# A graph attention kernel on one core: the last stage cut into 25 units, most of them run between the last steps of the edge loop

## The chip, the core and the metric

The kernel runs on one core of a Trainium2 chip. Its engines are TensorE (PE in the profile, its weight loads PEld), VectorE (DVE), ScalarE (ACT), GpSimd (POOL) and SyncE (SP), each with its own instruction stream, worked off in order. SyncE, ScalarE and GpSimd also issue DMA transfers, which 16 DMA engines carry out. The metric is the device time of one execution, in microseconds, as a median of several.

## The reference

There are 12,500 nodes with 128 features and 400,000 edges, sorted by their target node. Node rows are normalized, cut at zero, and multiplied by two weight matrices. Each edge adds the rows of its source and target, multiplies them by a small network's output on its 32 edge features and by its weight, and gives eight attention scores and eight value vectors. A softmax over all edges of a target weighs the values, which are summed per target, projected, and added to x:

```
h = maximum(layernorm(x), 0)
message = (h @ w_src + b_src)[src] + (h @ w_dst)[dst]
message = (message * edge_weight * mlp(edge_attr)) @ w_sep + b_sep
score = einsum(smooth_leaky_relu(message[:, :, :16]), alpha_dot)
att = exp(score - max[dst]) / (sum of exp over the target's edges + 1e-16)
out = segment_sum(message[:, :, 16:] * att, dst)
return x + out @ w_proj + b_proj
```

## The kernel before

**Node stage.** The rows of x are normalized and multiplied, and the tables t_src and t_dst are written to memory. The function fits checks that the targets are sorted and that no section of 512 edges spans more than 63 targets; its result, bad, chooses between the fast path (windows) and a slow one that never runs on these inputs.

**Edge loop.** In windows a step k handles two sections of 512 edges; there are NP = 391 steps. GpSimd gathers source rows two steps ahead. Transposes, the network, the message and the scores follow. The softmax needs maxima over eight steps, so the values are made LAG = 13 steps later: for c = k - 13, values multiplies and weighs, one_hot builds a selection matrix, and sums adds each section's edges into its window of 64 targets (tile ob, three buffers). store_win writes the whole window of a step to win; store writes 63 rows of each of its two sections to agg, at the row where the section's first target lies. So a step has three such transfers on SyncE's queue. Rows of targets that lie on a section's border come from several sections. They are joined by the block functions: a block takes the 128 border rows of 64 sections out of win (block_rows, tile rr), scales and adds them along the sections (block_maxima to block_totals), and block_out writes the joined rows to obs_d. There are NC = 13 blocks. The first eleven are made within the loop; the last two in the last steps. scatter lets GpSimd write joined rows to agg by an indirect transfer. The order of all this is written out by hand: each engine gets its instructions in the order of the program, and the program only adds the waits.

**The last steps.** Steps 391 to 404 hold what the lag leaves: values, sums and stores of c = 378 to 390, and the last two blocks by the table jobs. Here also the joined rows of the eleven early blocks are loaded from obs_d (tile comb, two buffers), one in each step, and scattered. A store to agg waits for the stores and scatters before it, and a scatter for the stores, since rows may overlap; only stores of the last block's sections (c from 384) are freed from waiting for scatters (declare_no_dep, group "combined"). From step 394 on ScalarE's queue loads x plus bias (xb, made during the loop) into one large tile x_fin, in 7 groups and a rest.

**The final stage.** The function final begins when all is scattered. agg is seen as 97 tiles of 128 nodes and a rest of 84, with node p * 97 + t on partition p. load_g loads agg by twelve tiles (128 partitions of 12 x 136 numbers), quotients divides the sums by the eight totals, turn transposes four tiles and copies them, finish multiplies them by w_proj, adds x_fin and writes the output.

Of the kernel before, what the change touches and what calls it, by code (L numbers as in the profile page):

```python
# [30 lines left out]
P = 128  # L31
C = 128
# [24 lines left out]
def gnn_kernel(ctx: ExitStack, tc: tile.TileContext, a: dict, out: bass.AP):  # L57
# [9 lines left out]
    NX = -(-NP // MP) * MP * PR  # L67
    assert NT * P == E and RC * RP == E and NT % TPI == 0 and NT % SORT_T == 0
# [88 lines left out]
    with tc.tile_pool(name="node", bufs=2) as np_, tc.tile_pool(name="node1", bufs=1) as n1, \  # L157
# [22 lines left out]
        ends = n1.tile([NH, 17, 2], I32, name="ends")  # L180
        eb = n1.tile([P, NS, 2], I32, name="eb")
# [6 lines left out]
        def load_targets():  # L188

            nc.sync.dma_start(out=cur[:, 1:CC + 1], in_=dst.rearrange("(p c) -> p c", p=P))  # L190
            at = dst[CC - 1:CC]
            with nc.allow_non_contiguous_dma(reason="single targets"):
                nc.sync.dma_start(out=cur[1:P, 0:1], in_=bass.AP(at.tensor, at.offset, [[CC, P - 1], [1, 1]]))
                at = dst[0:1]
# [114 lines left out]
        def fits():  # L309
# [14 lines left out]
            nc.vector.tensor_copy(bad, sum_)  # L324
# [425 lines left out]
    def windows():  # L750
# [7 lines left out]
        with tc.tile_pool(name="ps", bufs=1, space=PSUM) as pp, \  # L758
# [326 lines left out]

            def store(c, f):
                at = nc.sync.value_load(base[0:1, f, c:c + 1])
                st = nc.sync.dma_start(out=agg[ds(at, W - 1), :], in_=accs[c][f * W:(f + 1) * W - 1, :])
                if 2 * c + 1 >= (NC - 1) * (P // 2):
                    tc.declare_no_dep(st.ins, group="combined", reason="its rows follow those of the blocks")  # L1090
# [102 lines left out]
            def scatter(g):  # L1193
                w = width(g)
                st = nc.gpsimd.indirect_dma_start(
                    out=agg[0:N, :], in_=comb[g][:w, :], in_offset=None,
                    out_offset=bass.IndirectOffsetOnAxis(ap=ids[:w, g:g + 1], axis=0),
                    bounds_check=N - 1, oob_is_err=False)
                tc.declare_no_dep(st.ins, group="combined", reason="each node's row is written once")
                tc.add_to_no_dep_group("combined", st.ins)  # L1200

            comb = {}

            def combined(g):
                comb[g] = tail_pool.tile([P, ROW], F32, name="comb", bufs=2)
                return comb[g]
# [12 lines left out]
            def step(k):  # L1219
# [109 lines left out]

            for k in range(-5, NP):  # L1330
                step(k)
            held.close()


            tail_pool = held.enter_context(tc.tile_pool(name="fin1", bufs=1, side="right"))
            x_fin = tail_pool.tile([P, NB, C], F32, name="x_fin")
            x_loads = load_xb(x_fin)
            last = NC - 1

            def out_rows(g):  # L1340
                block_rows_out(g, combined(g))
                scatter(g)

# [9 lines left out]
                10: lambda: out_rows(last - 1),  # L1353
            }
            assert SB * (NC - 1) + LAG + 1 == NP + 7
            for k in range(NP, NP + LAG + 1):
# [4 lines left out]
                if 0 <= j - 2 < NC - 2:  # L1361
                    nc.sync.dma_start(out=combined(j - 2), in_=obs_d[(j - 2) * P:(j - 1) * P, :])
                    scatter(j - 2)
                if j >= 3:
                    next(x_loads, None)
            for _ in x_loads:
                pass
            block_rows(last)
# [4 lines left out]
            with tc.tile_pool(name="fin", bufs=3) as fp:  # L1373
                final(fp, x_fin, lambda i: pp.tile([P, 4, P], F32, name=("pm0", "pm1", "V")[i % 3]),
                      lambda i: pp.tile([P, 4, C], F32, name=("p3", "pa", "m1")[i % 3]))


    XQ = 12
    out_v = out[0:NF * P, :].rearrange("(p t) c -> p t c", t=NF)
    agg_v = agg[0:NF * P, :].rearrange("(p t) c -> p t c", t=NF)  # L1380

    def load_xb(x_fin):

        for t0, t1 in groups:
            nc.scalar.dma_start(out=x_fin[:, t0:t1, :], in_=xb_v[:, t0:t1, :])
            yield
        nc.scalar.dma_start(out=x_fin[:tail, NF, :], in_=xb[NF * P:N, :])
        yield

    def final(fp, x_fin, turned, product):  # L1390
        starts = list(range(0, NB, XQ))
        gs, qs, qTs = {}, {}, {}

        def load_g(i):

            gs[i] = fp.tile([P, XQ, ROW], F32, name="g", bufs=len(starts))
            for n, t0, t1 in blocks(starts[i], min(starts[i] + XQ, NB)):
                o = starts[i]
                nc.sync.dma_start(out=gs[i][:n, t0 - o:t1 - o, :],
                                  in_=agg_v[:, t0:t1, :] if n == P else agg[NF * P:N, :].unsqueeze(1))  # L1400

        def quotients(i):
            r = fp.tile([P, XQ, H], F32, name="r")
            qs[i] = fp.tile([P, XQ, C], F32, name="q")
            g = gs.pop(i)
            for n, t0, t1 in blocks(starts[i], min(starts[i] + XQ, NB)):
                s = slice(t0 - starts[i], t1 - starts[i])
                m = t1 - t0
                nc.vector.tensor_scalar(r[:n, s, :], g[:n, s, C:ROW], 1e-16, None, op0=ALU.add)  # L1409
                nc.vector.reciprocal(r[:n, s, :], r[:n, s, :])  # L1410
                nc.vector.tensor_mul(  # L1411
                    qs[i][:n, s, :].rearrange("p t (h k) -> p (t h) k", h=H),
                    g[:n, s, 0:C].rearrange("p t (h k) -> p t h k", h=H),
                    r[:n, s, :].unsqueeze(3).to_broadcast([n, m, H, C // H]))

        def turn(i):
            t0, t1 = quads[i]
            q, o = qs[t0 // XQ], t0 // XQ * XQ
            pt = turned(i)
            for t in range(t0, t1):  # L1420
                n = rows(t)
                nc.tensor.transpose(pt[:, t - t0, :n], q[:n, t - o, :], ident[:n, :n])  # L1422
            w = (t1 - t0 - 1) * P + rows(t1 - 1)
            qTs[i] = fp.tile([P, 4, P], F32, name="qT")
            nc.scalar.copy(qTs[i].rearrange("p u n -> p (u n)")[:, :w], pt.rearrange("p u n -> p (u n)")[:, :w])

        def finish(i):
            t0, t1 = quads[i]
            qT = qTs.pop(i)
            py = product(i)  # L1430
            for t in range(t0, t1):
                n = rows(t)
                nc.tensor.matmul(py[:n, t - t0, :], qT[:, t - t0, :n], w_proj, start=True, stop=True)  # L1433
            for n, u0, u1 in blocks(t0, t1):
                y = x_fin[:n, u0:u1, :]
                nc.vector.tensor_add(y, py[:n, u0 - t0:u1 - t0, :], y)  # L1436
                nc.sync.dma_start(out=out_v[:, u0:u1, :] if n == P else out[NF * P:N, :].unsqueeze(1), in_=y)

        for i in range(len(starts)):
            load_g(i)  # L1440
        quotients(0)
        turn(0)
        for i in range(Q):
            if i % 3 == 1 and i // 3 + 1 < len(starts):
                quotients(i // 3 + 1)
            if i + 1 < Q:
                turn(i + 1)
            finish(i)

# [4 lines left out]
    with fit.Else():  # L1454
# [23 lines left out]
        with tc.tile_pool(name="fin_b", bufs=3) as fp, tc.tile_pool(name="fin1_b", bufs=1) as f1, \  # L1478
                tc.tile_pool(name="fin_ps", bufs=2, space=PSUM) as fps, tc.manual_schedule():
            x_fin = f1.tile([P, NB, C], F32, name="x_fin")  # L1480
            for _ in load_xb(x_fin):
                pass
            final(fp, x_fin, lambda i: fps.tile([P, 4, P], F32, name="pt"),
                  lambda i: fps.tile([P, 4, C], F32, name="py"))
# [36 lines left out]
```

## Time and profile before

| | us |
|---|---|
| median of 3 runs | 4215.05 (4213.84 to 4223.81) |
| the profiled execution | 4210.53 |
| its span, first to last instruction | 4208.8 |
| busy in it: PE, DVE, ACT, POOL | 3913.5, 3104.8, 1901.2, 3010.2 |

A row of the stretches gives busy time and count of instructions of each engine, then the granted clock of TensorE, the busy share of the 16 DMA engines and what they moved. A row of waits names who waited for whom, the sum in us, how often, and the longest. A row of the timeline gives start, duration, engine and line, operation, out<-in, and in brackets the idle time before it with what ended it; SPq is SyncE's queue, whose rows are DMA issues. Where a row says x2, it spans from the first issue to the end of the second.

### The profile page before, as it was taken

What the parts mean: (1) busy time and instruction counts of PE and PEld (TensorE: products, weight loads), DVE (VectorE), ACT (ScalarE), POOL (GpSimd) and SP (SyncE); (2) the same over time, 40 slices, a digit from 0 to 9 for tenths busy, and PEclk for the clock granted to TensorE, in tenths of its full rate; (3) what the DMA queues carried; (4) which work ended last, traced back from release to release, by engine and by line L of the source; (5) the groups of instructions that cost most, each with busy time, mean ns of one, the idle gap of its engine ahead of it and who ended that gap; (6) DMA issues with size and microseconds to landing.
All of it is one profiled execution on the core that took longest, in us unless ns stands there. A gap on an engine that the chain in (4) does not pass through costs nothing. (4 is left out here: it accounts for less than half of the span.)

```text
span 4208.8 us, 87885 instructions
## 1 busy us (share of the span) xinstructions
PE 3913.5 (93%) x29351; PEld 2388.5 (57%) x29351; DVE 3104.8 (74%) x6187; ACT 1901.2 (45%) x4549; POOL 3010.2 (72%) x3195
## 2 busy tenths in 40 slices
PE   6889999999999999999999999999999999999975
PEld 5345555555555555555555555555555555555554
DVE  5567777777777777777777777777777777777754
ACT  5344444444444444444444444444444444444421
POOL 4777777777777777777777777777777777777710
PEclk8899999999999999999999999999999999999988
DMA  6767776777776776777777776676677776766634
GB/s 238 235 181 183 187 193 178 197 192 180 198 193 178 197 194 185 189 197 190 184 192 192 181 194 185 177 188 183 178 187 187 185 183 181 189 179 182 184 86 161
DMA packets 593333, 783.08 MB, mean 186 GB/s; under 512 B 125553, under 2 KB 392302, under 8 KB 592740
## 3 DMA queue, kind: packets, MB, share of 16 engines
q1 hardware_dynamic: 384786, 514.16, 40.6%
q0 software_dynamic: 100416, 205.44, 23.9%
q10 hardware_dynamic: 107666, 57.76, 4.7%
q8 instruction: 234, 3.83, 0.4%
q14 instruction: 231, 1.89, 0.1%
HBM read 637.83 MB, written 139.30 MB: 185 GB/s over the span
## 5 line engine op out<-in xcount | busy, mean ns | idle before, releaser
L865 POOL DMA_INDIRECT gs<-t_src,idx x3125 | 2972.3, 951 | 969.2 <-issue 807.5
L954 ACT ACTIVATE sl<-pa,c_b_a 128x512 f32<-128x512 f32 x782 | 536.9, 687 | 1018.6 <-PE pa L952 1009.9
L959 DVE SCALAR_TENSOR_TENSOR al<-pa,sl 128x512 f32<-128x512 f32 x782 | 540.5, 691 | 594.3 <-ACT sl L954 582.9
L1063 PEld LDWEIGHTS V<-c_w_v,mT 128*128 128x128 f32 x6048 | 746.8, 194 | 292.3 <-DVE ob L1080 119.1
L1063 PE MATMUL V<-c_w_v,mT 128*128 128x128 f32 x6048 | 879.4, 289 | 0.0
L952 PE MATMUL pa<-mT,c_w_a 128*128 128x512 f32 x1564 | 814.0, 603 | 3.9 <-DVE mT L946 3.6
L1065 DVE TENSOR_TENSOR pvx<-V,Pem 128x512 f32<-128x512 f32 x756 | 519.2, 687 | 243.4 <-PE V L1063 230.3
L932 PEld LDWEIGHTS pm<-ident,gs 128*128 128x128 f32 x3125 | 393.3, 142 | 420.4 <-issue 289.6
L1076 PEld LDWEIGHTS misc<-pvx,oh 128*64 128x64 f32 x6250 | 352.5, 137 | 410.6 <-ACT h L888 394.3
L924 DVE SCALAR_TENSOR_TENSOR rad<-p,c_fc_b,w_b 128x512 f32<-128x512 f32 x782 | 550.3, 745 | 39.4 <-PE p L916 3.7
L1076 PE MATMUL misc<-pvx,oh 128*64 128x136 f32 x6250 | 453.8, 287 | 118.3 <-ACT h L888 108.3
L946 DVE SCALAR_TENSOR_TENSOR mT<-pm,c_b_src,rad 128x512 f32<-128x512 f32 x782 | 550.7, 746 | 4.8 <-PE pm L939 4.8
L902 ACT ACTIVATE h<-p,b 128x512 f32<-128x512 f32 x391 | 287.5, 735 | 419.8 <-PE p L899 369.1
L932 PE MATMUL pm<-ident,gs 128*128 128x128 f32 x3125 | 471.9, 274 | 0.0
L916 PE MATMUL p<-h,w3b 64*128 64x512 f32 x1564 | 405.4, 595 | 11.5 <-ACT h L902 11.5
L939 PE MATMUL pm<-ohT,m 64*128 64x512 bf16 x2346 | 323.3, 382 | 0.0
L985 ACT ACTIVATE Sp<-m,b_s 128x512 f32<-128x512 f32 x192 | 131.9, 687 | 394.2 <-PE m L968 394.2
L884 PE MATMUL m<-eT,w1b 64*128 64x256 f32 x782 | 274.4, 431 | 26.1 <-DVE M L1006 16.7
L884 PE MATMUL misc<-eT,w1b 64*128 64x256 f32 x782 | 274.4, 431 | 0.0
L1049 DVE TENSOR_TENSOR oh<-lane,misc 128x504 f32<-128x504 f32 x391 | 262.3, 671 | 0.0
L899 PE MATMUL p<-h,w2b 64*64 64x256 f32 x3128 | 259.8, 403 | 0.0
L952 PEld LDWEIGHTS pa<-mT,c_w_a 128*128 128x128 f32 x1564 | 241.9, 195 | 21.2 <-DVE mT L946 8.1
(172 smaller groups left out, 3649.1 us busy)
## 6 DMA issues: line engine op xcount, KB each, us to landing
w_b<-in_edge_weight SPq DMA_DIRECT2D x390, 512.0 KB
d_b<-in_dst SPq DMA_DIRECT2D x390, 256.0 KB
gs<-t_src,idx POOLq DMA_INDIRECT x3125
e_t<-in_edge_attr ACTq DMA_DIRECT2D x390, 128.0 KB
sc_d<-Sp SPq DMA_DIRECT2D x192, 256.0 KB
win<-ob SPq DMA_DIRECT2D x391, 68.0 KB
agg<-ob SPq DMA_DIRECT2D x782, 33.5 KB
md<-t_dst SPq DMA_DIRECT2D x782, 32.0 KB
```

The lines of the kernel that those rows point to most:

```text
L865: nc.gpsimd.indirect_dma_start(out=gs[:, t, :], out_offset=None, in_=t_src[:, :], in_offset=bass.IndirectOffsetOnAxis(ap=idx[:, t0 + t:t0 ...
L884: nc.tensor.matmul(p1[q], w1b[s, :], eTs[k][s, :], start=True, stop=True)
L916: nc.tensor.matmul(p3s[k][:, f, 0:SEC], w3b[s, :], h2s[k][s, :], start=True, stop=True)
L924: nc.vector.scalar_tensor_tensor(rad[:, s], p3[:, f, 0:n], b3, w_g[k][:, s], op0=ALU.add, op1=ALU.mult)
L932: nc.tensor.matmul(pms[k, f][:, t * T:(t + 1) * T], gs[:, t, :], ident, start=(t == 0), stop=False, is_transpose=True, skip_group_check=True)
L946: nc.vector.scalar_tensor_tensor(mTs[k][:, s], pms.pop((k, f))[:, 0:n], b_n, rad[:, s], op0=ALU.add, op1=ALU.mult)
L952: nc.tensor.matmul(pa[:, 0:n], w_a, mTs[k][:, f * SEC:f * SEC + n], start=True, stop=True)
L954: nc.scalar.activation(sl[:, 0:n], pa[:, 0:n], AF.Silu, bias=b_a, scale=1.0)
L959: nc.vector.scalar_tensor_tensor(al, pa, 0.25, sl, op0=ALU.mult, op1=ALU.add)
L1063: nc.tensor.matmul(V[:, t, :], mTs[c][:, o:o + T], w_v, start=True, stop=True)
L1065: nc.vector.tensor_mul(pvx[c][:, f, 0:n, 0:C].rearrange("p t (h k) -> p t h k", h=H), V[:, 0:n, :].rearrange("p t (h k) -> p t h k", h=H), ...
L1076: nc.tensor.matmul(acc[f * W:(f + 1) * W, :], ohs[c][:, f * TS + t, :], pvx[c][:, f, t, :], start=(t == 0), stop=(t == n - 1), skip_group_ ...
```

## The change

The final stage becomes 25 units of 500 nodes (class Units). Unit u takes nodes 500 u to 500 u + 499, node 500 u + 4 p + t on partition p, so 125 partitions with four nodes each. For a unit, load_x loads 125 x 512 numbers of x plus bias, load_g 125 x 544 numbers of agg, quotients divides in place, turn transposes and copies, finish multiplies, adds and writes 125 x 512 numbers. x has eight buffers and is loaded three units ahead, g has nine and is loaded up to eight ahead. x and the output go over SyncE's queue, and g over ScalarE's for the first 23 units and SyncE's for the last two.

- 18 of the units run in steps 393 to 404, one and two in turn, behind each step's stores and block work. Two more stand between the last block's parts, three behind its scatter, and two at the very end.
- The joined rows of the eleven early blocks are loaded in steps 385 to 388 (bring), three blocks at a time, into buffers of the edge features that are no longer needed, and all eleven scatters are issued at the end of step 388, behind the last gather.
- order replaces the one group by four. Stores and scatters are sorted by section into three classes (below section 704, below 768, the rest), and one class doesn't wait for another's; units below 20 wait for the first class alone, units 20 to 22 for the first two. Two targets are read from dst in the node stage (lim), and fits sends inputs to the slow path where units 0 to 19 or 0 to 22 could hold nodes of later sections.
- In the last step the last window isn't written to win; two rows of each of its sections' borders go from ob to rr directly (last_rows, last_rows_2).

```diff
+            low = n1.tile([1, 2], F32, name="low")
+            for i, u in enumerate((EARLY_1, EARLY)):
+                nc.vector.tensor_scalar(low[:, i:i + 1], lim[:, i:i + 1], float(u * (N // NU)), None, op0=ALU.is_lt)
+            nc.vector.tensor_add(sum_, low[:, 0:1], sum_)
+            nc.vector.tensor_add(bad, low[:, 1:2], sum_)
...
                 if has(c - 1):
                     sums(c - 1)
                     if k >= NP:
-                        store_win(c - 1)
+                        if k == NP + LAG:
+                            last_rows_2()
+                        else:
+                            store_win(c - 1)
                         store(c - 1, 0)
                         store(c - 1, 1)
...
             for k in range(-5, NP):
                 step(k)
+                if 0 <= k - (NP - 6) < 4:
+                    bring(k - (NP - 6))
+                if k == NP - 3:
+                    for g in range(NC - 2):
+                        scatter(g)
...
+            def last_rows_2():
+                q = width(last) // 2
+                for i in range(2):
+                    nc.sync.dma_start(out=rrs[last][(i + 1) * q - 2:(i + 1) * q, :],
+                                      in_=accs[NP - 1][i * (W - 1):i * (W - 1) + W + 1:W, :])
...
-                if 0 <= j - 2 < NC - 2:
-                    nc.sync.dma_start(out=combined(j - 2), in_=obs_d[(j - 2) * P:(j - 1) * P, :])
-                    scatter(j - 2)
-                if j >= 3:
-                    next(x_loads, None)
...
+                if j == 0:
+                    un.load_x(0, 3)
+                    for u in range(7):
+                        un.load_g(u)
+                if j == 1:
+                    un.quotients(0)
+                    un.quotients(1)
+                    un.turn(0)
+                if j >= 2:
+                    un.run(1 + j % 2, EARLY)
+            un.run(1, EARLY)
             block_columns(last)
+            un.run(1, EARLY)
             block_totals(last)
             out_rows(last)
+            un.run(NU, EARLY)
...
+            un.run(NU, NU)
...
+        def load_x(self, u0, u1):
+            for u in range(u0, min(u1, NU)):
+                self.x[u] = self.pool.tile([UP, UT, C], F32, name="xu", bufs=self.nx)
+                nc.sync.dma_start(out=self.x[u], in_=self.view(xb, u))
...
+        def load_g(self, u):
+            self.g[u] = self.pool.tile([UP, UT, ROW], F32, name="g", bufs=self.ng)
+            eng = nc.scalar if u < EARLY else nc.sync
...
+        def finish(self, u):
+            qT, py, y = self.qT.pop(u), self.product(u), self.x.pop(u)
+            for t in range(UT):
+                nc.tensor.matmul(py[:UP, t, :], qT[:, t, :], w_proj, start=True, stop=True)
+            nc.vector.tensor_add(y, py[:UP], y)
+            nc.sync.dma_start(out=self.view(out, u), in_=y)
...
+        def run(self, n, end):
+            for _ in range(n):
+                if self.nf >= end:
+                    return
+                u = self.nf
+                while self.ng_ < min(u + 8, end):
+                    self.load_g(self.ng_)
+                while self.nq < min(u + 3, end):
+                    self.quotients(self.nq)
+                while self.nt < min(u + 2, end):
+                    self.turn(self.nt)
+                self.finish(u)
+                self.load_x(u + 3, u + 4)
```

More of the change, by code (lines that the diff above doesn't have):

```diff
@@ L193, in load_targets @@
                 nc.sync.dma_start(out=cur[1:P, 0:1], in_=bass.AP(at.tensor, at.offset, [[CC, P - 1], [1, 1]]))
+                for i, s in enumerate(EARLY_S):
+                    nc.sync.dma_start(out=lim[:, i:i + 1], in_=dst[s * SEC:s * SEC + 1].unsqueeze(1))
                 at = dst[0:1]
@@ L1084, in store_win, with order @@
                 nc.sync.dma_start(out=win[c * P:(c + 1) * P, :], in_=accs[c])
+            def order(ins, s, whole=False):
+                i = 1 if s < EARLY_S[0] else 2 if s < EARLY_S[1] else 3
+                for j in (1, 2):
+                    if j < i:
+                        tc.declare_no_dep(ins, group=f"early_{j}", reason="its rows follow those of the earlier sections")
+                    if i <= j:
+                        tc.declare_no_dep(ins, group=f"later_{j}", reason="its rows precede those of the later sections")
+                if whole and i < 3:
+                    tc.add_to_no_dep_group(f"early_{i}", ins)
+                if i > 1:
+                    tc.add_to_no_dep_group(f"later_{i - 1}", ins)
             def store(c, f):
@@ L1088, in store @@
                 st = nc.sync.dma_start(out=agg[ds(at, W - 1), :], in_=accs[c][f * W:(f + 1) * W - 1, :])
-                if 2 * c + 1 >= (NC - 1) * (P // 2):
-                    tc.declare_no_dep(st.ins, group="combined", reason="its rows follow those of the blocks")
+                order(st.ins, 2 * c)
             def load_x(i):
@@ L1378, in gnn_kernel @@
[L1378 to L1448, printed above, removed]
@@ L1477, in gnn_kernel @@
               ea_s.rearrange("(t p) c -> p t c", p=P), "b")
[L1478 to L1484, printed above, removed]
+        with tc.tile_pool(name="fin_b", bufs=3) as fp, tc.tile_pool(name="fin_ps", bufs=2, space=PSUM) as fps, \
+                tc.manual_schedule():
+            un = Units(fp, 10, 10, lambda u: fps.tile([P, 4, P], F32, name="pt"),
+                       lambda u: fps.tile([P, 4, C], F32, name="py"))
+            un.load_x(0, 3)
+            un.run(NU, NU)
 def kernel(**inputs):
```

72 lines of the change are left out of this document (58 added, 14 removed).

## The prediction

> **What bounds the kernel now.** I read the busy time by stage first, then the waits of the tail, then its timeline on SyncE's queue. The last steps and the last stage, by stretches (busy time of PE, PEld, DVE, ACT and POOL, granted clock, DMA share, GB/s):
>
> ```profile
> 4040.00:4068.00 28.00, 23.22 (x207) 17.37 (x206) 17.76 (x39) 8.01 (x24) 0.10 (x1) 1.00 0.25 55
> 4068.00:4137.00 69.00, 31.92 (x246) 27.20 (x246) 20.50 (x56) 3.39 (x18) 11.76 (x13) 0.74 0.37 122
> 4137.00:4144.00 7.00, 0.00 (x0) 0.00 (x0) 0.00 (x0) 0.00 (x0) 0.76 (x1) 0.50 0.53 182
> 4144.00:4202.00 58.00, 38.85 (x294) 36.91 (x294) 38.52 (x56) 14.38 (x25) 0.00 (x0) 0.90 0.52 201
> ```
>
> Up to 4040 us the main loop runs with PE nearly always busy, and the change leaves that loop's arithmetic alone. From 4068 to 4137 no engine is busy even half the time: the ten last steps wait. Then come 7 us with nothing at all, and 58 us of the final stage. The waits say for whom:
>
> ```profile
> POOL agg L1195 <- DMA comb<-obs_d: 47.6, 9, 11.4
> ```
> ```profile
> SPq L1088 <- DMA agg<-comb,ids: 20.5, 4, 11.0
> SPq L1088 <- DMA agg<-ob: 18.3, 21, 3.6
> ...
> SPq L1399 <- DMA g<-agg: 2.1, 2, 1.8
> ```
>
> One turn of the ring, from the timeline:
>
> ```profile
> 4084.40 0.36 SPq L1362 DMA_DIRECT2D comb<-obs_d  x1
> 4084.81 0.42 SPq L1084 DMA_DIRECT2D win<-ob  x1
> 4087.01 0.97 POOL L1195 DMA_INDIRECT agg<-comb,ids  x1 [5.75 <-DMA comb<-obs_d]
> 4089.21 1.82 SPq L1088 DMA_DIRECT2D agg<-ob  x2
> ```
>
> A store of rows waits for the scatter before it, the scatter for its joined rows, and their load stands on SyncE's queue behind the store. Each turn takes about 7 us. Without the ring a step is short; two sums that follow each other freely are 3.0 us apart:
>
> ```profile
> 4121.24 0.30 DVE L1080 TENSOR_TENSOR ob<-misc,bare 128x136 f32<-128x136 f32 x1 [2.84 <-PE misc L1076]
> ...
> 4124.25 0.30 DVE L1080 TENSOR_TENSOR ob<-misc,bare 128x136 f32<-128x136 f32 x1 [0.42 <-PE misc L1076]
> ```
>
> **The change, part by part: small edits.** Two single-word loads and three more one-word VectorE operations in the prologue: bounded by 0 and 2 x 0.36 + 3 x 0.16 = 1.2 us (the issue of comb above, the shortest VectorE form below); I take 0, since the sum can't tell 1 us. Four loads of joined rows in the loop's last steps: 204 KB each, one issue of 0.36 us (the row of comb), beside gathers; between 0 and 2 us, I take 0. Eleven scatters behind the last gather:
>
> ```profile
> 4012.23 0.95 POOL L865 DMA_INDIRECT gs<-t_src,idx  x1 [0.30 <-issue]
> 4067.90 1.02 POOL L1195 DMA_INDIRECT agg<-comb,ids  x1 [54.73 <-PE misc L1076]
> ```
>
> GpSimd stands idle for 54.7 us there, so 11 x 1.25 us end near 4027, ahead of the first load of g (about 4050). They cost nothing, and the ring is gone. The last rows from SBUF save a store and a load, some 2 us, which lie beside three units of other work: taken as 0, at most 2. The x loads leave ScalarE and stand on SyncE's queue instead: 25 issues of about 0.35, and 23 of g on ScalarE.
>
> **The units, their arithmetic.** Work of the final stage by instruction:
>
> ```profile
> 4191.90 0.75 DVE L1410 RECIPROCAL r<-r 128x96 f32<-128x96 f32 x1
> 4192.68 1.76 DVE L1411 TENSOR_TENSOR q<-g,r 128x1536 f32<-128x1536 f32 x1
> ...
> 4197.48 0.69 DVE L1436 TENSOR_TENSOR x_fin<-p,x_fin 128x512 f32<-128x512 f32 x1 [0.64 <-PE p L1433]
> 4198.09 0.16 DVE L1409 TENSOR_SCALAR r<-g 128x8 f32<-128x8 f32 x1
> 4198.28 0.20 DVE L1410 RECIPROCAL r<-r 128x8 f32<-128x8 f32 x1
> 4198.52 0.29 DVE L1411 TENSOR_TENSOR q<-g,r 128x128 f32<-128x128 f32 x1
> ```
>
> Between the long and the short form, a unit's sizes (32 and 512 elements) come to 0.17 (little above the short form's 0.16) + 0.35 + 0.69 = 1.21 us of quotients, and 0.69 for the sum: 1.90 us of VectorE. 25 units are 47.5 us, where the stage now has 38.5: 9 us more work, but 18 units lie between the steps. If nothing else bound, VectorE would have its 20.5 us of steps and 47.5 us of units from 4068 on, 4136, and then some 5 us of handing over, the 7 us without work between last scatter and first quotient (third row of the stretches), 2.2 us of the last unit and 7.0 us of end: 4157, 52 us gained. That is the gain the arithmetic allows.
>
> **The units, their transfers.** Here is what I think decides. A unit is laid on 125 partitions, not 128: 2,048 bytes of x, 2,176 of g and 2,048 of output on each, 784,000 bytes in all. The kernel before has such a transfer already: z, on 125 partitions, 340,000 bytes.
>
> ```profile
> L133 POOL MEMSET z<- x1: 654/654/654, 1.5 to 1.5; 125x680 f32 x1
> ```
> ```profile
> 161.11 0.69 SPq L139 DMA_DIRECT2D agg<-z  x2
> ```
>
> Two of them are issued by 161.8 us. What the DMA engines do while they, and later ones, are moving, against loads of g and one output on 128 partitions:
>
> ```profile
> 168.00:168.50 0.50, 0.50 (x5) 0.23 (x6) 0.29 (x1) 0.37 (x1) 0.34 (x1) 0.50 0.38 127
> 180.50:181.00 0.50, 0.50 (x4) 0.25 (x3) 0.08 (x1) 0.00 (x0) 0.36 (x1) 1.00 0.34 131
> 4146.00:4150.00 4.00, 3.02 (x13) 2.79 (x14) 0.88 (x1) 1.17 (x2) 0.00 (x0) 0.50 1.01 423
> 4168.60:4169.40 0.80, 0.80 (x9) 0.80 (x9) 0.56 (x1) 0.07 (x1) 0.00 (x0) 1.00 0.87 326
> ```
>
> With 128 partitions all 16 engines are busy and 423 GB/s move. With 125, a share of 0.34 is busy, about five engines of 16, and 131 GB/s move, though more is queued: two in flight (168.0) don't take ten engines. So five engines carry a transfer of 125 partitions, the same five each time on this queue. At 131 GB/s x costs 1.95 us, g 2.08, the output 1.95: 5.98 us a unit, 150 us for 25 units, where compute needs 1.9. Whether ScalarE's queue (g) gets the same five no row tells: bounds 5.98 (same) and 3.9 (others, g beside). I take the same, by the nearest row, that of two z transfers.
> [...]
>
> **The sum.** SyncE comes to the first x load behind the load of the maxima, at 4051.5:
>
> ```profile
> 4050.82 0.64 SPq L1126 DMA_DIRECT2D mx<-max_d  x1
> ```
>
> Three x and seven g take 3 x 1.95 + 7 x 2.08 = 20.4 us: 4072. (Of the ten g loads of the stage now, two waited for loads of the same list, row above, so I read eight in flight; the store of step 1 waits behind these.) With 2 us for landing and issue the first output goes at 4074. Then each step holds one or two units and its two stores of rows. The second store waits for the first to land: 1.82 us for the pair with an empty queue (row of 4089.21). Now the first stands behind outputs and x loads, SyncE waits until they have drained, and the next outputs, though computed, aren't issued. So per step, beside the units: 0.5 us for its own stores (138 KB, between 0.3 at 423 GB/s and 1.1 at 131) and a gap of 1.5 us (1.82 less one issue), between 0 if g fills it and 1.8. Eleven steps with 16 units: 16 x 5.98 + 11 x 2.0 = 117.7, to 4192. Behind the last step 7 outputs and 6 x loads, 13 x 1.95 = 25.4: 4217. The last scatter lies beside this. The two late g loads on SyncE, 4.2 us and 0.6 to land: 4222. One unit's chain, 1.21 quotients, 0.60 transposes, 0.58 copy, 1.06 product, 0.69 sum: 4226. From the last sum to the end as now:
>
> ```profile
> 4196.38 1.06 PE L1433 MATMUL p<-c_w_proj,qT 128*128 128x128 f32 x8
> ...
> 4197.28 0.60 PE L1422 MATMUL V<-ident,q 128*128 128x128 f32 x4
> ...
> 4197.97 0.58 ACT L1425 COPY qT<-V 128x512 f32<-128x512 f32 x1 [0.74 <-PE V L1422]
> ...
> 4201.36 0.47 DVE L1436 TENSOR_TENSOR x_fin<-p,x_fin 128x128 f32<-128x128 f32 x2
> ```
>
> 4201.8 to 4208.8 is 7.0, so 4233: 24 us more than 4208.8. The profiled execution took 4210.53; the median of the runs shown, 4215.05, lies 4.5 above it. 4215 + 24 = 4239. Everything that was won from the ring and the final stage is lost to five engines.
>
> **Rivals.** (1) The transfers stay hidden: units on 125 partitions move like those on 128, at 423 GB/s 1.9 us a unit, beside compute. For it: their outer memory side is contiguous, that of z isn't. Against it: the partition side is the same. It decides if a unit's three transfers take under some 4 us. Then the 52 us stand: 4163, faster. (2) Five engines, but g fills every gap: 11 x 1.5 = 16.5 us less, 4223, +0.2%, the same. For it: g comes over another queue. Against it: seven to eight units of g are there early, so the gaps find that queue empty. (3) g goes on five other engines: 25 x 2.08 = 52 us off the five, of which the wait behind the stores keeps some 15: 4239 - 37 = 4202, faster by 0.3%. (4) Slower still: rows of 2 KB move worse than the 2.7 KB of z. Five sixteenths of 326 GB/s are 102, so 7.7 us a unit, 43 us more: 4282; against it, that row holds one transfer with its start and end. Or ScalarE, whose loads of g wait for a free place in flight, holds up its copies and with them the steps: some 20 us, 4259.
>
> **How the numbers follow.** The forecast has 0.52 (4226 to 4262 alone), (1) 0.14, (2) 0.14, (3) 0.07, (4) 0.13. About 0.3%, 12.6 us, is what a measurement can tell from no change. Slower: the forecast's 0.52 and (4)'s 0.13; same: (2) and half of (3), 0.17; faster: 0.18. The range leaves out (1) and the top of (4): 4200 to 4280.
>
> **What would show it.** Right: from 4055 to the end a DMA share of 0.3 to 0.4 and about 130 GB/s without a break; VectorE idle more than half of that; waits of the row stores on the row store before them, some 8 us each in about eleven steps, where 18.3 us stand now; no wait of a store on a scatter; scatters at 4013 to 4027. Wrong: a DMA share near 1 in bursts, or g landing in 2 us while x lands in 2 us beside it. If the stretch is DMA-bound but ends before 4225, the gaps were mis-sized; if VectorE is busy most of the time and the end lies near 4157, the five engines were wrong.

## The result, and the profile after

The changed kernel took 4280.34 us in the median (4275.48 to 4285.70), beside 4216.33 for the kernel before under the same conditions: a ratio of 1.0148, 95% interval 1.0135 to 1.0161, or 64 us slower. The forecast had the direction and the five engines, but 24 us instead of 64, and its range ended 0.3 us short of the measured median. The profiled execution took 4281.99 us, with a span of 4280.2.

First where the time lies. GpSimd's last gather and first scatter in the changed kernel, and the same rows in another execution of the same changed kernel (start, duration, engine and line, operation, tiles):

```profile
4024.78 0.94 POOL L875 DMA_INDIRECT gs<-t_src,idx  x1 [0.30 <-PE p L926]
4026.02 1.02 POOL L1216 DMA_INDIRECT agg<-e_t,ids  x1 [0.30 <-issue]
...
4038.86 0.97 POOL L1216 DMA_INDIRECT agg<-e_t,ids  x1 [0.31 <-issue]
```
```profile
4017.90 1.13 POOL L875 DMA_INDIRECT gs<-t_src,idx  x1 [0.30 <-PE pa L962]
```

The last gather stood at 4012.23 before. It comes 12.6 us later in the one execution of the changed kernel and 5.7 us later in the other, though no instruction of the main loop was changed. In four traces with the loop of before (before, ring and the two probes below) it starts at 4012.2 to 4014.9, in ten with the changed kernel's at 4011.1 to 4024.8, some 3 us later on average, so most of the 12.6 us is what executions differ by. So I count from the last gather. From there to the end of the span the kernel before takes 196.6 us and the changed one 255.4 (255.8 in its other execution): 58.8 us, and these lie in the last steps and behind them.

The last steps by stretches (busy time of PE, PEld, DVE, ACT and POOL, granted clock, DMA share, GB/s), and one of the late stretches:

```profile
4068.00:4100.00 32.00, 19.01 (x156) 17.08 (x157) 19.84 (x47) 6.88 (x19) 0.00 (x0) 0.76 0.32 102
4100.00:4137.00 37.00, 18.60 (x145) 16.54 (x143) 14.19 (x38) 2.56 (x10) 0.00 (x0) 0.79 0.32 106
4137.00:4180.00 43.00, 25.56 (x205) 23.42 (x205) 17.76 (x42) 4.84 (x16) 0.97 (x1) 0.79 0.34 106
4240.00:4260.00 20.00, 5.69 (x34) 5.47 (x34) 2.91 (x5) 1.42 (x3) 0.91 (x1) 0.67 0.33 127
```

The DMA share stands at 0.32 to 0.34 in these stretches, about five engines of 16, as forecast. But the forecast's other sign, about 130 GB/s without a break, isn't there: the GB/s are 102 to 106 in the steps, and 127 only in the last, late stretch. VectorE is busy 38% and 41% of the second and third stretch. SyncE's queue waits for row stores as forecast (line L1110 is the row store), nearly five times as long as the 18.3 us before:

```profile
SPq L1110 <- DMA agg<-ob: 89.1, 21, 10.8
```

No store waits for a scatter any more. One step on SyncE's queue, the first output of the last step, and the two late loads of g with what follows, from the timeline:

```profile
4090.07 0.28 SPq L1483 DMA_DIRECT2D out<-xu  x1
4090.39 0.34 SPq L1448 DMA_DIRECT2D xu<-xb  x1
4090.87 0.54 SPq L1094 DMA_DIRECT2D win<-ob  x1
4092.51 9.75 SPq L1110 DMA_DIRECT2D agg<-ob  x2
4102.35 0.28 SPq L1483 DMA_DIRECT2D out<-xu  x1
...
4230.16 0.28 SPq L1483 DMA_DIRECT2D out<-xu  x1
```
```profile
4252.95 2.21 SPq L1454 DMA_DIRECT2D g<-agg  x2
4263.81 0.18 DVE L1464 TENSOR_SCALAR r<-g 125x32 f32<-125x32 f32 x1 [11.27 <-DMA g<-agg]
...
4268.25 1.91 PE L1481 MATMUL m<-c_w_proj,qT 128*125 128x128 f32 x8
...
4269.96 1.72 PE L1481 MATMUL p<-c_w_proj,qT 128*125 128x128 f32 x8
...
4271.71 0.69 DVE L1482 TENSOR_TENSOR xu<-p,xu 125x512 f32<-125x512 f32 x1 [0.82 <-PE p L1481]
```

From 4090.07 to 4230.16, eleven steps with 16 units take 140.1 us. Two things had to be found out: whether five engines are the cause at all, and why a step takes longer than five engines explain.

### The profile page after: what moved, and what is told of

It reads as the page before. It is cut to its first block, busy times and chain, and to the rows that moved or that the text cites. A ratio compares the mean times of both kernels' runs of the same rounds, so it can differ in the third digit from the quotient of the medians.

```text
span 4280.2 us, 87976 instructions
## 1 busy us (share of the span) xinstructions
PE 3932.1 (92%) x29357; PEld 2404.1 (56%) x29357; DVE 3107.4 (73%) x6234; ACT 1901.6 (44%) x4549; POOL 3015.3 (70%) x3195
## 4 chain that ended last, share of the span: by engine, by line
PE 81%; DMA 6%; DVE 5%; ACT 4%; issue 2%; SPq 1%; ACTq 0%; DVEq 0%; POOL 0%
PE V L1073 17%; PE pa L962 15%; PE misc L1086 9%; PE pm L942 7%; PE p L926 7%; PE pm L949 7%; PE m L894 5%; PE m L978 5%; PE p L909 5%; PE m L885 2%; DMA agg<-ob 2%; DVE M L1021 1%; ACT L964 1%; DMA xu<-xb 1%; DMA w_b<-in_edge_weight 1%
```

## The experiments

**The partition count, two ways.** The units on 128 partitions (with 512 nodes each, so that the last overlaps the one before it, and 19 units instead of 20 in the first class):

```diff
-    UP, UT = 125, 4
+    UP, UT = 128, 4
...
-            return t[u * UN:(u + 1) * UN, :].rearrange("(p t) c -> p t c", t=UT)
+            n0 = min(u * UN, N - UN)
+            return t[n0:n0 + UN, :].rearrange("(p t) c -> p t c", t=UT)
```

> Units of 512 nodes on 128 partitions instead of 500 on 125 (the last one overlaps the one before it, and the two write parts that don't overlap); everything else as in the changed kernel. Theory (the five engines are the cause): the DMA share in the last steps leaves its plateau of 0.32, a unit's three transfers take about 1.9 us at 423 GB/s, VectorE's 20.5 us of steps and 48.6 us of units bind, and the time falls by 85 to 110 us, to 4170 to 4195, below the kernel before. Rival (the second row store's wait for the first, or SyncE's order of issue, is the cause, whatever the partitions): pairs of row stores still take 8 us or more, and the time stays above 4250.

And the units as they are, each transfer issued as two (the same in load_g and for the output):

```diff
-                nc.sync.dma_start(out=self.x[u], in_=self.view(xb, u))
+                for p0, p1 in ((0, 112), (112, UP)):
+                    nc.sync.dma_start(out=self.x[u][p0:p1], in_=self.view(xb, u)[p0:p1])
```

> The changed kernel with its 125 partitions, but each transfer of a unit is issued as two, of 112 and of 13 partitions: 75 issues more, same bytes, same rows, same layout. [...] Rival (the layout in memory or the order of issue binds): 4270 or more, since issues are only added.

Measured beside 4218.05 us for the kernel before: 128 partitions 4181.16 us (ratio 0.9917, 0.9900 to 0.9933), split transfers 4193.87 (0.9947, 0.9930 to 0.9964). Both lie far below the 4250 and 4270 of the rivals, and the first in the range of its theory. The stretches with 128 partitions, then one with split transfers:

```profile
4068.00:4100.00 32.00, 28.36 (x260) 25.93 (x258) 24.78 (x59) 7.06 (x22) 0.00 (x0) 0.94 0.60 156
4100.00:4140.00 40.00, 34.18 (x307) 30.74 (x303) 33.83 (x83) 7.84 (x24) 0.97 (x1) 0.96 0.66 210
```
```profile
4068.00:4100.00 32.00, 28.30 (x256) 25.85 (x254) 24.03 (x55) 6.98 (x22) 0.00 (x0) 0.93 0.58 144
```

The plateau is gone, the DMA share is 0.6, and VectorE is busy 77% and 85% of the two stretches: arithmetic has come close to binding. The split kernel has the layout, the rows and the order of the slow one; the only difference is that a transfer is cut into 112 and 13 partitions. So the partition count costs 86 to 99 us, more than the whole loss of 64, and the rest of the change is a gain. How many engines carry the 112 and the 13 no run shows; the share of that stretch is 0.58.

**The disputed cost by itself.** Behind the output of the kernel before, groups of four transfers in flight, each group waiting for the one before:

```diff
+                for p in (128, 125, 126, 124, 120, 100, 64):
+                    move([(0, p)], 4, [SPq])
+                move([(0, 112), (112, 125)], 4, [SPq])
+                move([(0, 125)], 4, [SPq, ACTq])
+                move([(0, 128)], 4, [SPq, ACTq])
+                move([(0, 125)], 4, [POOLq])
...
+                move([(3, 128)], 4, [SPq])
+                move([(0, 125)], 8, [SPq])
...
+                move([(0, 125)], 4, [SPq], xb, True)
```

> The kernel before with transfers measured by themselves behind its output (its time is longer by these): four transfers in flight of p partitions with 2,048 bytes each, one group after the other. [...] Rows of 4,096 and 2,720 bytes: by a fixed price per row 15 to 20% more GB/s than rows of 2,048, by bytes alone the same. Rival (the plateau is no matter of the partition count): 128 and 125 partitions within 20% of each other.

VectorE's small memset ends each group, and its wait is the group's time with issue and landing. In order: 128, 125, 126 and 124 partitions; 112 + 13; 125 on SyncE's and ScalarE's queues in turn:

```profile
4216.95 0.06 DVE L1390 MEMSET row<- 128x4 f32 x1 [5.96 <-DMA row<-xb]
4227.89 0.06 DVE L1390 MEMSET row<- 128x4 f32 x1 [10.88 <-DMA row<-xb]
4234.28 0.06 DVE L1390 MEMSET row<- 128x4 f32 x1 [6.33 <-DMA row<-xb]
4247.23 0.06 DVE L1390 MEMSET row<- 128x4 f32 x1 [12.89 <-DMA row<-xb]
...
4269.68 0.06 DVE L1390 MEMSET row<- 128x4 f32 x1 [6.04 <-DMA row<-xb]
4280.44 0.06 DVE L1390 MEMSET row<- 128x4 f32 x1 [10.70 <-DMA row<-xb]
```

The middle of some groups as stretches (last two columns: DMA share, GB/s): 125 on SyncE's queue, 124, 125 on both queues, 125 on GpSimd's, partitions 3 to 127, 125 with rows of 4,096 bytes, 125 stored:

```profile
4220.00:4225.00 5.00, 0.00 (x0) 0.00 (x0) 0.00 (x0) 0.00 (x0) 0.00 (x0) 0.50 0.33 127
4237.00:4245.00 8.00, 0.00 (x0) 0.00 (x0) 0.00 (x0) 0.00 (x0) 0.00 (x0) 0.50 0.26 101
4273.00:4278.00 5.00, 0.00 (x0) 0.00 (x0) 0.00 (x0) 0.00 (x0) 0.00 (x0) 0.50 0.33 129
4288.50:4291.50 3.00, 0.00 (x0) 0.00 (x0) 0.00 (x0) 0.00 (x0) 0.13 (x1) 0.50 0.88 264
4305.00:4310.00 5.00, 0.00 (x0) 0.00 (x0) 0.00 (x0) 0.00 (x0) 0.00 (x0) 0.50 0.33 129
4316.00:4328.00 12.00, 0.00 (x0) 0.00 (x0) 0.00 (x0) 0.00 (x0) 0.00 (x0) 0.50 0.32 131
4373.00:4378.00 5.00, 0.00 (x0) 0.00 (x0) 0.00 (x0) 0.00 (x0) 0.00 (x0) 0.50 0.33 127
```

124 partitions are slower than 125 (12.89 us against 10.88) and 126 nearly as fast as 128 (6.33 against 5.96); two queues move no more than one (0.33 and 129 GB/s, where five other engines beside would give about 0.66), so SyncE and ScalarE share the same five engines, which the trace of before could not show. Rows of 2,048 bytes move nearly as fast as those of 4,096 (127 and 131), and stores, once under way, as fast as loads (127): the reason that rival (4) gave doesn't hold. A share of 0.33 is about five engines of 16, 0.26 about four, and 0.88 on GpSimd's queue most of the 16; for 126 there are only its 6.33 us. What sets the number of engines for a partition count, and which of the sixteen the five are, no row here shows.

**The ring alone.** The kernel before with the loads of joined rows in the loop and the scatters behind the last gather, the final stage left as it was:

```diff
                 step(k)
+                if 0 <= k - (NP - 6) < 4:
+                    bring(k - (NP - 6))
+                if k == NP - 3:
+                    for g in range(NC - 2):
+                        scatter(g)
...
-                    nc.sync.dma_start(out=combined(j - 2), in_=obs_d[(j - 2) * P:(j - 1) * P, :])
-                    scatter(j - 2)
```

> The kernel before with one part of the change: the joined rows loaded within the loop and the eleven scatters behind the last gather; the final stage, x and the last rows stay as they were. Theory (the ring of store, scatter and load is worth what its stretch shows): steps fall from 7 us to 3 to 4, and the time by 30 to 35 us, to 4180 to 4186. Rival (the last block's chain of loads and joins sets the pace of the last steps anyway): under 15 us, above 4200.

4205.31 us (0.9973, 0.9962 to 0.9984): 12.7 us, the rival's side. This version lacks the change's four groups, and there a row store still waits for the eleven scatters, once:

```profile
SPq L1088 <- DMA agg<-e_t,ids: 15.3, 1, 15.3
```

The first load of the last two blocks' targets is issued 44.6 us behind the last gather in it, and 38.1 to 39.5 us in the three traces with the whole kernel before; so the ring may be worth 5 to 6 us more than 12.7, still far from 30. Without the ring, other transfers end the waits of the last steps; from its timeline (in brackets the idle time and what ended it):

```profile
4082.81 0.30 DVE L1080 TENSOR_TENSOR ob<-misc,bare 128x136 f32<-128x136 f32 x1 [3.09 <-DMA agg<-ob]
...
4093.81 0.19 DVE L1139 TENSOR_TENSOR differ<-node 128x28 bf16<-128x28 int32 x1 [9.44 <-DMA node<-ends_d]
...
4103.36 0.30 ACT L1163 COPY rx<-rr 128x128 f32<-128x128 f32 x1 [5.52 <-DMA rr<-win]
```

These are a row store that still held a buffer of ob, and the loads of the last blocks' targets and rows. The ring's stretch looked like 30 us because the ring hid them. That it pays when there are units to put into these waits is my reading; no run has the units with the ring.

**ScalarE's share taken off the five engines.** The changed kernel with the g loads of units 0 to 18 on GpSimd's queue; its other line makes a scatter wait for earlier scatters and the early loads of g, from which it was freed:

```diff
-                    if j < i:
+                    if j < i and not whole:
...
-            eng = nc.scalar if u < EARLY else nc.sync
+            eng = nc.gpsimd if u < EARLY_1 - 1 else nc.scalar if u < EARLY else nc.sync
```

> The changed kernel (125 partitions), with the g loads of units 0 to 18 issued by GpSimd instead of ScalarE. In the transfers measured by themselves GpSimd's queue spread 125 partitions over all engines (share 0.88). Theory: 19 x 2.13 = 40 us leave the five engines, some of it into the waits behind the row stores: 25 to 40 us less, 4240 to 4255, and ScalarE is no longer blocked for 8 us ahead of the steps. Rival (g, beside x and outputs, wasn't what the five engines lacked time for): 4270 or more.

4255.93 us beside 4215.88 (1.0100, 1.0083 to 1.0117), where the changed kernel stands at 1.0148: about 20 us by the ratios, 24 by the medians, a little under the 25 to 40 expected, and why not more stays open. This is the forecast's rival (3) built on purpose, with 19 of its 25 loads.

**Why a step takes so long: first a poor test.** The second row store behind the step's units:

```diff
                         store(c - 1, 0)
-                        store(c - 1, 1)
+                        second.append(c - 1)
...
                     un.run(1 + j % 2, EARLY)
+                    store(second.pop(), 1)
```

> The changed kernel (125 partitions), but from the third of the last steps on a step's second row store is issued behind its units, no longer right behind the first, so that the first has landed by then. Theory (a step costs more than its units because SyncE waits for the first store's landing while nothing new is issued): 1.5 to 3 us less in each of eleven steps, 16 to 33 us, 4247 to 4264. Rival (the five engines have work queued during that wait, and their bytes alone set the pace): within 5 us of the changed kernel's 4280.

4275.40 us (1.0142, 1.0125 to 1.0159): by the numbers the rival's side. But the waits of its row stores say that the edit only moved the wait. The next step's first row store now waits for the second one, which stands behind the same outputs:

```profile
SPq L1110 <- DMA agg<-ob: 92.8, 21, 12.6
```

So it tells nothing apart.

**The transfers of the steps without the steps.** Behind the output of the kernel before, streams of 16 units' transfers without computation, x and outputs on SyncE's queue, g on ScalarE's, and once with a step's three row transfers after each second unit, to constant places:

```diff
+                    for i in range(n):
+                        if o:
+                            nc.sync.dma_start(out=view(xb, 8 + i, q), in_=one[:q, 0:512])
+                        if x:
+                            nc.sync.dma_start(out=row[:q, i % 8, 0:512], in_=view(xb, i % 8, q))
+                        if g:
+                            nc.scalar.dma_start(out=tot[:q, i % 8, :], in_=view(agg, i % 8, q))
...
```

> The kernel before, and behind its output streams of transfers of a unit's kinds without any computation (its time is longer by these): 16 x loads on 125 partitions, 16 outputs, both in turn on SyncE's queue, x on SyncE's with g on ScalarE's, all three, all three with a step's three row transfers after each second unit (constant places, no waits for each other), and the last two with 128 partitions. Theory (the mixture itself is slower on the five engines than the forecast's 131 GB/s): x alone 127 to 129 GB/s, outputs alone 115, all three 100 to 110, with the row stores 98 to 106, as in the last steps of the changed kernel. Rival (the five engines stand idle in the steps because of waits): all mixtures 120 or more, and the steps' 98 to 106 come from idle time.

All three kinds, and all three with rows, by stretches, and the memsets that ended each (the wait is the group's time):

```profile
4425.00:4518.00 93.00, 0.00 (x0) 0.00 (x0) 0.00 (x0) 0.00 (x0) 0.00 (x0) 0.50 0.33 127
4526.00:4624.00 98.00, 0.00 (x0) 0.00 (x0) 0.00 (x0) 0.00 (x0) 0.00 (x0) 0.50 0.35 133
```
```profile
4522.14 0.07 DVE L1398 MEMSET row<- 128x8 f32 x1 [102.58 <-DMA row<-xb]
...
4628.11 0.07 DVE L1398 MEMSET row<- 128x8 f32 x1 [105.67 <-DMA agg<-one]
```

The mixture isn't slow: 127 to 133 GB/s, 102.58 / 16 = 6.41 us a unit with the stream's start and landing, and (105.67 - 102.58) / 8 = 0.39 us for a step's rows. The other streams of 125 partitions moved at 124 to 128 GB/s. My theory of a slower mixture fell. On 128 partitions the two streams shown took 34.92 and 41.98 us. Eleven steps with 16 units would take 16 x 6.41 + 11 x 0.39 = 106.9 us; the changed kernel takes 140.1. So 33 us, 3.0 a step, come from the steps themselves.

**The wait taken away.** From the third of the last steps on, the row stores go to places of their own, so that none waits for another; the rows of these sections are missing from agg:

```diff
-                        store(c - 1, 0)
-                        store(c - 1, 1)
...
+                                s = 2 * (k - NP) + f
+                                nc.sync.dma_start(out=aside[s * W:s * W + W - 1, :],
+                                                  in_=accs[c - 1][f * W:(f + 1) * W - 1, :])
```

> The changed kernel (125 partitions), but from the third of the last steps on the two row stores of a step go to places of their own in a buffer beside agg, in the same size and with the same reading of the place's register. So no row store waits for another; left out are the rows that these sections give to agg, so the last nodes' output is not theirs. Alone, a step's transfers take 6.41 us a unit and 0.4 us for its rows, 107 us for eleven steps with 16 units, and the changed kernel takes 140.1. Theory (SyncE's wait for the first store drains the five engines, and that and the start after it cost 3.0 us a step): 25 to 36 us less, 4244 to 4255. Rival (the loss is in the sharing of places in flight with ScalarE's queue, or in computing beside): under 8 us less, 4272 or more.

It took 5338.33 us beside 5317.10 for the kernel before (1.0050, 1.0032 to 1.0067): both took a quarter longer than elsewhere. The trace kept shows it in the unchanged main loop (from 1000 to 2000 us PE is busy 810 us, in the kernel before 963), and what disturbed it is open, so this result can't be set against 4280. The same kernel again, with the changed kernel itself beside it:

> The same kernel as in free once more, because in that run the kernel before took 5317 us, not 4216, in its unchanged loop. From the third of the last steps on the row stores go to places of their own beside agg; left out are these rows of agg. Theory (the wait drains the five engines): eleven steps in 105 to 112 us instead of 140.1, and 25 to 36 us less than the changed kernel's 4280. Rival: steps above 130 us, and under 8 us less.

> The changed kernel as it is, beside free2 on the same chip, so that the two are compared under the same conditions. Both theories: 1.013 to 1.016 of the kernel before, and 140 us for the eleven steps, if the chip runs the loop in its usual time.

Without the wait 4247.63 us, the changed kernel 4277.46, the kernel before 4219.19 (1.0067, 1.0047 to 1.0088, against 1.0137, 1.0117 to 1.0158): 29.8 us, as the theory had it. The row stores' waits without it (those of the steps ahead), first output of the first and of the last of the eleven steps, and two stretches:

```profile
SPq L1111 <- DMA agg<-ob: 12.2, 6, 6.9
```
```profile
4080.75 0.28 SPq L1490 DMA_DIRECT2D out<-xu  x1
...
4189.23 0.43 SPq L1490 DMA_DIRECT2D out<-xu  x1
```
```profile
4100.00:4137.00 37.00, 22.92 (x145) 20.00 (x143) 17.34 (x46) 4.46 (x16) 0.00 (x0) 0.68 0.37 136
4137.00:4180.00 43.00, 28.08 (x226) 24.70 (x224) 21.43 (x51) 5.49 (x15) 0.97 (x1) 0.87 0.36 135
```

Eleven steps in 108.5 us, near the 106.9 of the bare transfers, at 135 GB/s. So nearly the whole step overhead goes with the wait of a row store for the one before it. That these rows now go beside agg isn't what helps: in the streams above they went into agg, beside loads of agg, at 133 GB/s.

**Versions that beat both.** On 128 partitions, with the second row store behind the units; with the first loads ahead of the first of the last steps and the units a step earlier; and with both:

```diff
                 j = k - NP
+                if j == 0:
+                    un.load_x(0, 3)
+                    for u in range(7):
+                        un.load_g(u)
+                step(k)
...
-                if j >= 2:
+                if j >= 1:
```

> Units on 128 partitions, and the second row store behind the units. SyncE waits 26.9 us for row stores in the 128-partition kernel. Theory (by now VectorE, busy 0.77 to 0.85 of the steps, sets the pace): 0 to 6 us less, 4175 to 4182. Rival (SyncE's wait still holds up the outputs and x loads, and with them the units): 10 to 25 us less, 4156 to 4171.

> Units on 128 partitions; the first loads of x and g go ahead of the first of the last steps, and units run from the second of them on, a step earlier. VectorE is busy 15.5 of 28 us between 4040 and 4068 there. Theory (units fill this idle time): 4 to 10 us less than 4181. Rival (the loads stand ahead of the maxima's on SyncE's queue and ahead of copies on ScalarE, and delay the steps by what they gain): 4179 to 4190.

> Units on 128 partitions, with the early first loads and the second row store behind the units together. Each alone came to 4176, 5 below the 4181 of 128 partitions alone, which 3 rounds can hardly tell. If the two gains are real and add up: 4168 to 4174. If they are the same time, or none: 4175 to 4181.

4176.04 (0.9909, 0.9893 to 0.9926), 4176.27 (0.9911, 0.9893 to 0.9929) and 4175.09 (0.9905, 0.9888 to 0.9921). They can't be told from one another, nor from 128 partitions alone at 0.9917. All four beat the kernel before by 0.8 to 1.0%.

## Why the prediction was right or wrong

Its sum, term by term, counted from the last gather:

| | forecast | measured | difference |
|---|---|---|---|
| to the first output | 61.8 | 65.3 | +3.5 |
| eleven steps, 16 units | 117.7 | 140.1 | +22.4 |
| the outputs behind them, to the issue of the late g | 25.4 | 22.8 | -2.6 |
| the two late units, to the last sum | 8.9 | 19.4 | +10.5 |
| from the last sum to the end | 7.0 | 7.8 | +0.8 |
| in all | 220.8 | 255.4 | +34.6 |

**The five engines: right.** That 125 partitions are carried by five engines, and the same five on both queues (0.33 on one queue and on two), was the step that decided. Both ways of undoing it gain 86 us or more. The evidence that I had was thinner than it looked: the two rows of before for 125 partitions are half microseconds of a stretch in which other loads ran too, and from 167 to 169 us the share is 0.46, 0.60, 0.38 and 0.70. The transfers by themselves are what shows it. Rival (1) is out, and so is (3): with ScalarE's queue beside SyncE's no more than 0.33 was busy, and 129 GB/s moved. Rival (2), a g that fills every gap, is out as well: the gaps cost more than forecast.

**The price of a unit: a little low.** 5.98 us were taken from z's 131 GB/s; a stream of all three kinds moves at 127, so 6.17 us a unit. That is 3.1 of the 22.4 us in the steps. A step's rows took 0.39 us instead of 0.5, 1.2 us less in all.

**The gap behind the row stores: the term that was mis-sized.** "A gap of 1.5 us (1.82 less one issue), between 0 if g fills it and 1.8" was the landing of one store on an empty queue. With the wait, in the changed kernel beside free2, the first outputs of the first and of the last of the eleven steps stand here:

```profile
4084.96 0.28 SPq L1483 DMA_DIRECT2D out<-xu  x1
...
4223.62 0.28 SPq L1483 DMA_DIRECT2D out<-xu  x1
```

That is 138.7 us, against 108.5 without the wait: 30.2 us, 2.7 a step, where 16.5 were forecast. The 1.8 that I had set as the upper bound was too low. My working priced the store's landing, but nothing behind it: that the queue moves slowly when it starts again stood in the sum at nothing. One step of the changed kernel, where SyncE's wait for the first store ends near 4183.0 and the next output goes at 4183.04, and the first us of the stream of all three kinds without computation:

```profile
4181.50:4183.00 1.50, 0.00 (x0) 0.00 (x0) 1.50 (x6) 0.00 (x0) 0.00 (x0) 0.87 0.06 20
4183.00:4186.50 3.50, 1.60 (x8) 1.63 (x9) 1.73 (x5) 0.58 (x1) 0.00 (x0) 0.50 0.30 50
4187.00:4195.00 8.00, 4.98 (x34) 4.02 (x32) 1.82 (x4) 0.00 (x0) 0.00 (x0) 0.71 0.35 131
```
```profile
4420.00:4424.50 4.50, 0.00 (x0) 0.00 (x0) 0.00 (x0) 0.00 (x0) 0.00 (x0) 0.50 0.30 69
```

The queue runs empty while the store lands (20 GB/s), and then 3.5 us pass at 50 GB/s before it is 131 again. The stream without computation starts the same way, with 69 GB/s for 4.5 us. I added up stretches of half a microsecond over the eleven steps: in the changed kernel beside free2, 7 us lie below 10 GB/s and 38.5 us between 10 and 100, at 54 in the mean; without the wait these are 1.0 and 7.5 us. What moved in the 38.5 us would take 16.4 at 127 GB/s, so the slow starts cost 22 us, 2.0 a step. Only 0.7 us a step passed with the queue empty, where I had 1.5 for the gap; the larger part, the start behind it, was missing. Where loads of g were just issued, as beside the outputs of 4102.35, the rate holds better: 131 GB/s in the 3.5 us from there, 115 from 4116.78 and 108 from 4198.05. In the other eight steps of that execution the 3.5 us from the first output have 43 to 80 GB/s. Why a start is slow, no run shows.

The 22.4 us are then 3.1 for the rate, less 1.2 for the rows, 13.7 for the gap (30.2 less 16.5), 5.4 by which free2 too lies above its bytes at full rate (it begins and ends with an empty queue), and 1.4 between the two executions of the changed kernel.

**The late units: the second term.** I let the two late g loads start when SyncE issues them. At 4252.95 they are issued, at 4263.81 used, 10.9 us later instead of 4.8. At 127 GB/s (the stretch from 4240) 10.9 us are 1.38 MB, and the two loads are 0.54 MB; by this estimate three earlier transfers still stood in the queue. And it is 8.6 us from there to the last sum, instead of one unit's 4.1: two units in turn, with products of 1.91 and 1.72 us where 1.06 was taken. With 128 partitions the same stretch, from issue to last sum, still takes 10 us, so about half of it has nothing to do with the five engines:

```profile
4162.72 0.90 SPq L1455 DMA_DIRECT2D g<-agg  x2
...
4172.07 0.69 DVE L1483 TENSOR_TENSOR xu<-p,xu 128x512 f32<-128x512 f32 x1 [0.20 <-PE p L1482]
```

**What was costed at nothing: right.** The eleven scatters end 15 us behind the last gather's start, as forecast (4027 against 4012.2), and 18 us ahead of the first load of g. No store of the changed kernel waits for them, as one did in the ring kernel. What the prologue's and the loop's small edits cost lies within the spread between executions, 3 us by the mean of the last gathers. ScalarE was held up once by its g loads, as rival (4) had it:

```profile
4058.06 8.00 ACTq L1454 DMA_DIRECT2D g<-agg  x7
4066.10 0.34 ACT L1053 COPY pvx<-Pem 128x32 f32<-128x32 f32 x2 [7.67 <-DMA g<-agg]
```

Eight us of queue, of which the first output shows at most the 3.5 of the table (5.3 in the other execution). Rival (4) named 4282 as its time, which is nearly what came, but by luck: it had it from rows of 2 KB that move worse, and these do not.

**The gain of the arithmetic: right in kind.** The forecast had 52 us if nothing but VectorE bound; with 128 partitions 37 to 42 came. The ring "is gone" held, but alone it gave 12.7 us.

## What to carry to other kernels

Before a tile gets another partition count than 128, look for a transfer with that count in the trace and set its DMA share against one of 128: 125 cost 86 to 99 us here, more than everything that the change won, and cutting each transfer into 112 + 13 got most of it back without a change of layout. When a store must wait for the one before it on a queue that carries bulk transfers, price not only the landing (I took 1.5 us) but also the slow start of the queue behind it (both together 2.7 us a step here), and look whether the wait disappears or only moves to the next store. What a stretch with a wait in it is worth shows only when something is ready to take its place: the ring filled 69 us, and its removal gave 12.7 by itself.

## What the runs showed of the hardware that was not expected

A stream of bulk transfers started slowly here, and the DMA share doesn't show it. On 125 partitions the stream of all three kinds moved at 69 GB/s for its first 4.5 us (share 0.30) and at 127 after that (0.33); four stores alone moved at 115 GB/s from 2 to 7 us behind their first issue (0.32) and at 127 from 4 to 9 us (0.33). In the changed kernel's steps the share is 0.32 at 102 to 106 GB/s. So only the GB/s tell, in stretches short enough to keep a start apart from what follows; why the engines count as busy in a slow start no row shows.

A transfer of 125 partitions moves at 127 GB/s on SyncE's queue, at 129 on SyncE's and ScalarE's in turn, and at 264 on GpSimd's. 124 partitions move at 101, and four transfers of 126 take 6.33 us where four of 125 take 10.88: in these groups one partition more or fewer matters more than which partitions (3 to 127: 129 GB/s) or how long a row is (131 at twice the length).
